# Norm scale and shift, and the MLP's 96x96 weight, computed by GpSimd instead of VectorE

## The chip, the cores and the metric

The kernel runs on one core of one Trainium2 chip. The metric is the device time of one execution in microseconds (us), lower is better. The chip's engines in the profile are PE (TensorE matmul), PEld (its weight loads), DVE (VectorE), ACT (ScalarE), POOL (GpSimd) and SP (SyncE, which here issues the DMAs). Each engine works through its own instructions in order; semaphores hold an instruction back until what it needs is done.

## The reference

Four residual layers on an image batch x of 8 x 48 x 48 x 96, all in float32. Ahead of each stands a group norm with 32 groups of 3 channels:

```python
def _gn(v, G=32, eps=1e-5):
    B_, H_, W_, C_ = v.shape
    g = v.reshape(B_, H_, W_, G, C_ // G)
    m = jnp.mean(g, axis=(1, 2, 4), keepdims=True)
    s = jnp.var(g, axis=(1, 2, 4), keepdims=True)
    return ((g - m) / jnp.sqrt(s + eps)).reshape(v.shape)

x = x + L0(_gn(x))   # selective scan in four directions over the image
x = x + L1(_gn(x))   # upsample, MLP 96 -> 384 -> 96 with a quadratic, low-pass, downsample
x = x + L2(_gn(x))   # four selective scans, each along single rows or columns
x = x + L3(_gn(x))   # as L0, with other weights
return x
```

A selective scan keeps 16 states for each of 192 channels, h = exp(dt A) h + dt u B, and its output is the sum over the states of h C. It is most of the work: 4 directions x 192 channels x 16 states x 2304 positions for each image in each of three layers.

## The kernel before, in words

The batch's images go one after another through three stages that run on the whole core: `ss2d` for layer 0 ("l0", to about 5.9 ms), `lines` for layer 2 (to about 11.9 ms) and `ss2d` for layer 3 ("l3"). Layer 1, the MLP, has no stage of its own. It is a guest (class `Guest`): a generator of small steps that is given a turn in each slot of the scans of l0 and lines, when it has a free PSUM bank.

A stage is driven by `scans`. For each image and each of four directions it goes through five blocks of 480 or 384 positions. A block has four turns of two slots; a turn makes three scans of two units each. The order of the instructions is written out by hand. In a turn t the emission is:

- `scan(t, 0)` on VectorE (L331), the recurrence in place in the tile dbu, with the decays ps_da in PSUM;
- on GpSimd the second product h times C of the turn before (`make_hc`, L337);
- products dt u B for the next turn (`make_dbu`, L299), on VectorE with a copy of B in PSUM (ps_b, copied by ScalarE in L280), and for certain slots a share of them on GpSimd with B in SBUF (bc);
- `scan(t, 1)`, more of the same, then `aside(at)`, which runs the slot's side work;
- `make_hc(t, 0)` on GpSimd, `make_da` (ScalarE's exponentials, L323, into two ps_da buffers), `scan(t, 2)`, and `aside(at + 1)`.

TensorE sums h C over the states (`reduce`, L357 and L359). Side work is what `aside` takes from the generators: the next image's norm and convolution, the finish of the image before, the first projections of later blocks, and the guest's turn.

The norm of an image is `norm_scale` (called by `group_norm` in l0 and l3, whose ScalarE application is L177, and by `front` in lines, application L809). It has six `bn_stats` (L191), one `bn_aggr` (L195), a matmul with gmat that takes the mean over the three channels of a group (L186), a copy of that mean out of PSUM to gm (L200), then dev = (mean - gm)^2 + variance (L202 to L204), seven slots later the same matmul on dev, ScalarE's square root to rs (L210), the reciprocal (L212), and shift = -gm rs (L214). All of dev, gm, rs and shift are 96 partitions by one column. It runs once for each image and stage, 24 times; the first of each stage runs before the stage's scans begin. The guest has its own norm for each of 8 images: gm copied by ScalarE (L1125), `deviate` (L1113 to L1115), the root (L1130), and `invert` (L1118 reciprocal, L1119 shift, L1120 the 96x96 matrix wl = wlin rs + I, which is used some 700 us later and more). A guest's step that is a "psum" item puts a matmul and the reader of its result; "do" runs a step, "wait" skips slots.

Tiles whose names begin with ps lie in PSUM; the others named here lie in SBUF.

Of the kernel before, what the change touches and what calls it, by code (L numbers as in the profile page):

```python
# [11 lines left out]
ALU = mybir.AluOpType  # L12
# [3 lines left out]
H, W, C = 48, 48, 96  # L16
# [85 lines left out]
def vss_stack_kernel(ctx: ExitStack, tc: tile.TileContext, i: dict, out: bass.AP):  # L102
    nc = tc.nc
# [11 lines left out]
    def weights(pool, names):  # L115
        w = {}
        for name in names:
            shape = list(i[name].shape)
            w[name] = pool.tile(shape, F32, tag=f"w_{name}", name=f"w_{name}")
            nc.sync.dma_start(w[name], i[name])  # L120
        return w

    wc = weights(const, ("gmat", "red"))
# [44 lines left out]
        return t  # L168


    def group_norm(x, into, psum, behind=lambda step: step()):


        got = {}
        yield from norm_scale(x, got, psum, behind)
        for r0, nr in BLKS:
            nc.scalar.activation(into(r0, nr), x[:, r0:r0 + nr, :], AF.Identity, bias=got["shift"], scale=got["rs"])  # L177
            yield True

    def norm_scale(x, got, psum, behind=lambda step: step()):  # L180


        def mean_of(v):
            def run():
                got["p"] = psum()
                nc.tensor.matmul(got["p"][:C, :1], lhsT=wc["gmat"], rhs=v, start=True, stop=True)  # L186
            behind(run)

        st = small.tile([C, 6, nc.vector.BN_STATS_DIM], F32, tag="st", name="st")
        for n in range(6):  # L190
            nc.vector.bn_stats(st[:, n, :], x[:, 8 * n:8 * n + 8, :])  # L191
            if n % 2:
                yield True
        mv = small.tile([C, 2], F32, tag="mv", name="mv")
        nc.vector.bn_aggr(mv, st)  # L195
        yield True
        mean_of(mv[:, 0:1])
        yield
        gm = small.tile([C, 1], F32, tag="gm", name="gm")
        nc.vector.tensor_copy(gm, got["p"][:C, :1])  # L200
        dev = small.tile([C, 1], F32, tag="dev", name="dev")
        nc.vector.tensor_sub(dev, mv[:, 0:1], gm)  # L202
        nc.vector.tensor_mul(dev, dev, dev)
        nc.vector.tensor_add(dev, dev, mv[:, 1:2])  # L204
        for _ in range(7):
            yield True
        mean_of(dev)
        yield
        rs = small.tile([C, 1], F32, tag="rs", name="rs", bufs=2)
        nc.scalar.activation(rs, got["p"][:C, :1], AF.Sqrt, bias=eps5[:C])  # L210
        yield True
        nc.vector.reciprocal(rs, rs)  # L212
        shift = small.tile([C, 1], F32, tag="shift", name="shift", bufs=2)
        nc.vector.scalar_tensor_tensor(shift, gm, -1.0, rs, ALU.mult, ALU.mult)  # L214
        got["rs"], got["shift"] = rs, shift
        yield True

# [292 lines left out]
    def ss2d(l, xin, xout, guest=None):  # L510
# [46 lines left out]
        def front(b):  # L557
            x = xpad[:C, 1:1 + H, 1:1 + W]
            yield from group_norm(x, lambda r0, nr: xpad[:C, 1 + r0:1 + r0 + nr, 1:1 + W], side_psum)
# [213 lines left out]
    def lines(xin, xout, guest):  # L773
# [29 lines left out]
        def front(b, behind=lambda step: step(), wait=()):  # L803
            got = {}
            x = seq(xs[b], False)
            yield from norm_scale(x, got, lambda: ps("sb", 1), behind)
            yield from wait
            for r0, nr in BLKS:
                nc.scalar.activation(shift(rowwise, 0, 0)[:C, r0:r0 + nr, :], x[:, r0:r0 + nr, :], AF.Identity,  # L809
                                     bias=got["shift"], scale=got["rs"])  # L810
                yield True
# [175 lines left out]
    class Guest:  # L987
# [54 lines left out]
        def items(self):  # L1042
# [5 lines left out]
            wlin, wl, bl = self.tile([C, C], "wlin"), self.tile([C, C], "wl"), self.tile([C, 1], "bl")  # L1048
            st, mv = self.tile([C, 6, nc.vector.BN_STATS_DIM], "st"), self.tile([C, 2], "mv")
            gm, dev, rs, shift = (self.tile([C, 1], n) for n in ("gm", "dev", "rs", "shift"))  # L1050
# [46 lines left out]
            for b in range(nb):  # L1097
# [11 lines left out]
                def mean_of(v):  # L1109
                    return lambda p: nc.tensor.matmul(p[:C, :1], lhsT=wc["gmat"], rhs=v, start=True, stop=True)  # L1110

                def deviate():
                    nc.vector.tensor_sub(dev, mv[:, 0:1], gm)  # L1113
                    nc.vector.tensor_mul(dev, dev, dev)
                    nc.vector.tensor_add(dev, dev, mv[:, 1:2])  # L1115

                def invert():
                    nc.vector.reciprocal(rs, rs)  # L1118
                    nc.vector.scalar_tensor_tensor(shift, gm, -1.0, rs, ALU.mult, ALU.mult)  # L1119
                    nc.vector.scalar_tensor_tensor(wl, wlin, rs, wc["ident"], ALU.mult, ALU.add)  # L1120

                def load_xt(c0):
                    nc.sync.dma_start(xt, self.xin[b].rearrange("c (h w) -> h c w", w=W)[:, c0:c0 + HC, :])

                yield "psum", mean_of(mv[:, 0:1]), lambda p: nc.scalar.copy(gm, p[:C, :1])  # L1125
                yield "do", lambda: load_xt(0)
                yield "wait", 1
                yield "do", deviate
# [221 lines left out]
```

## Time and profile before

| what | value |
|---|---|
| median of 3 runs | 17480.02 us (17457.32 to 17484.61) |
| the profiled execution | 17467.17 us |
| its span | 17465.4 us |
| mean granted TensorE clock | 0.839 |
| matmuls / instructions | 53740 / 168933 |
| VectorE instructions | 9976 |
| GpSimd instructions | 8015 |

The page of the profile gives for each engine the busy time, its share of the span and the number of instructions. A group line gives the source line, the engine, the operation, the tiles written and read, the shape, a count, then busy us and mean ns of one, and after the bar the idle us of the engine just ahead of these instructions with what ended that idle time. A table of stretches gives start and end, the length, and the busy us and instructions of PE, PEld, DVE, ACT and POOL, then the granted clock, the DMA engines' busy share and GB/s. A timeline line gives start us, length in us, engine, line, operation, tiles, shape and how many instructions are merged in it.

The page's waits show where each engine is held: ScalarE's L323 has 2436.5 us of idle time ahead of it, 2202.9 of it ended by VectorE's scans.

### The profile page before, as it was taken

What the parts mean: (1) busy time and instruction counts of PE and PEld (TensorE: products, weight loads), DVE (VectorE), ACT (ScalarE), POOL (GpSimd) and SP (SyncE); (2) the same over time, 40 slices, a digit from 0 to 9 for tenths busy, and PEclk for the clock granted to TensorE, in tenths of its full rate; (3) what the DMA queues carried; (4) which work ended last, traced back from release to release, by engine and by line L of the source; (5) the groups of instructions that cost most, each with busy time, mean ns of one, the idle gap of its engine ahead of it and who ended that gap; (6) DMA issues with size and microseconds to landing.
All of it is one profiled execution on the core that took longest, in us unless ns stands there. A gap on an engine that the chain in (4) does not pass through costs nothing.

```text
span 17465.4 us, 168933 instructions
## 1 busy us (share of the span) xinstructions
PE 13240.6 (76%) x53740; PEld 4749.1 (27%) x53740; DVE 15969.0 (91%) x9976; ACT 13903.6 (80%) x20972; POOL 15179.8 (87%) x8015
## 2 busy tenths in 40 slices
PE   6778787878787677777777777776777777777776
PEld 1223232333232333233233322222222222222221
DVE  7999999999999799899889999996999999999998
ACT  6878878878787688888788888886878878878776
POOL 7988888988888788888788888886999999999998
PEclk7878888888897888899889888887878878878877
DMA  4554555454555444444444444443555555455454
GB/s 139 179 169 167 174 166 175 169 177 168 165 176 172 135 147 162 147 158 156 153 154 155 153 155 156 153 157 125 173 174 171 176 168 178 171 170 177 169 177 145
DMA packets 887918, 2843.65 MB, mean 163 GB/s; under 512 B 353468, under 2 KB 421788, under 8 KB 760206
## 3 DMA queue, kind: packets, MB, share of 16 engines
q1 hardware_dynamic: 887022, 2832.85, 47.7%
q8 instruction: 422, 6.91, 0.2%
q14 instruction: 474, 3.88, 0.1%
HBM read 2384.40 MB, written 448.17 MB: 162 GB/s over the span
## 4 chain that ended last, share of the span: by engine, by line
DVE 22%; ACT 21%; POOL 19%; issue 14%; PE 13%; DMA 10%; SPq 1%; POOLq 0%; DVEq 0%; ACTq 0%
DVE dbu L331 14%; POOL dbu L337 12%; ACT ps_da L323 7%; DVE dbu L299 6%; POOL dbu L299 5%; DMA dd<-dds 4%; DMA dd<-dd 3%; ACT L323 3%; PE ps_y L357 2%; POOL dds L499 2%; ACT ps_b L280 1%; PE ps_sa L940 1%; PE ps_sa L885 1%; DMA bc<-bcd 1%; ACT L903 1%
## 5 line engine op out<-in xcount | busy, mean ns | idle before, releaser
L331 DVE TENSOR_TENSOR_SCAN dbu<-ps_da,dbu 128x968 f32<-128x968 f32 (+3 forms) x5760 | 11825.2, 2075 | 770.4 <-ACT ps_da L323 610.2
L337 POOL TENSOR_TENSOR dbu<-dbu,bc 128x1440 f32<-128x1440 f32 (+1 forms) x3840 | 10064.7, 2633 | 1941.7 <-DVE dbu L331 1860.2
L323 ACT ACTIVATE ps_da<-dd,w_l_a 128x484 f32<-128x484 f32 (+3 forms) x11520 | 7426.2, 649 | 2436.5 <-DVE dbu L331 2202.9
L357 PE MATMUL ps_y<-dbu,w_red 128*32 128x480 f32 (+1 forms) x23040 | 4253.3, 658 | 1600.6 <-POOL dbu L337 1572.4
L359 PE MATMUL ps_y<-dbu,w_red 128*32 128x480 f32 (+1 forms) x7680 | 4215.2, 657 | 0.0
L299 DVE TENSOR_TENSOR dbu<-dd,ps_b 128x962 f32<-128x962 f32 (+5 forms) x2880 | 3831.5, 1330 | 265.6 <-ACT ps_b L280 156.1
L299 POOL TENSOR_TENSOR dbu<-dd,bc 128x481 f32<-128x481 f32 (+5 forms) x2240 | 3911.2, 1761 | 23.6 <-DMA dd<-dd 19.0
L357 PEld LDWEIGHTS ps_y<-dbu,w_red 128*32 128x32 f32 x23040 | 729.0, 118 | 5033.5 <-POOL dbu L337 3369.4
L280 ACT COPY ps_b<-bc 128x482 f32<-128x482 f32 (+3 forms) x2720 | 1449.2, 533 | 214.7 <-DVE dbu L299 167.3
L574 PE MATMUL ps_side<-xpad,w_l_cw 128*128 128x480 f32 (+1 forms) x2880 | 1342.0, 604 | 48.4 <-ACT g_room L1176 16.9
L323 ACT ACT_TABLE_LOAD x993 | 1274.0, 1283 | 17.8
L703 PE MATMUL ps_s<-bcl,square 128*128 128x480 f32 (+1 forms) x1280 | 888.0, 785 | 323.2 <-ACT dds L707 163.8
L353 PE MATMUL ps_y<-big,eye 128*128 128x480 f32 (+1 forms) x960 | 748.3, 868 | 231.8 <-ACT big L754 227.4
L713 PE MATMUL ps_s<-big,square 128*128 128x480 f32 (+1 forms) x1280 | 849.4, 794 | 65.4 <-ACT g_room L1176 18.5
L499 POOL TENSOR_TENSOR dds<-dds,big 96x960 f32<-96x960 f32 (+1 forms) x320 | 705.9, 2206 | 166.6 <-ACT dds L731 166.2
L574 PEld LDWEIGHTS ps_side<-xpad,w_l_cw 128*128 128x128 f32 x2880 | 570.4, 209 | 804.9 <-issue 696.6
L885 PE MATMUL ps_sa<-ub,square 128*128 128x480 f32 (+1 forms) x640 | 405.0, 770 | 382.9 <-ACT ub L875 382.9
L359 PEld LDWEIGHTS ps_y<-dbu,w_red 128*32 128x32 f32 x7680 | 666.7, 118 | 0.0
L866 PE MATMUL ps_sb<-xpad,square 128*128 128x480 f32 (+1 forms) x1280 | 600.5, 615 | 85.0 <-ACT g_room L1176 31.3
L866 PE MATMUL ps_sa<-xpad,square 128*128 128x480 f32 (+1 forms) x1280 | 538.0, 561 | 0.0
L707 ACT ACTIVATE dds<-ps_s,w_l_dtb 96x480 f32<-96x480 f32 (+1 forms) x640 | 405.1, 633 | 123.4 <-DMA dd<-dds 71.0
L754 ACT COPY big<-ps_y 96x480 f32<-96x480 f32 (+1 forms) x640 | 471.0, 736 | 34.7 <-PE ps_y L359 33.3
(243 smaller groups left out, 12648.2 us busy)
## 6 DMA issues: line engine op xcount, KB each, us to landing
dd<-dd SPq DMA_DIRECT2D x512, 1452.0 KB
bc<-bcd SPq DMA_DIRECT2D x1536, 480.0 KB
dd<-dd SPq DMA_DIRECT2D x256, 1440.0 KB
dd<-dds SPq DMA_DIRECT2D x512, 363.0 KB
dd<-dd SPq DMA_DIRECT2D x128, 1164.0 KB
bc<-bcd SPq DMA_DIRECT2D x384, 384.0 KB
dd<-dds SPq DMA_DIRECT2D x256, 360.0 KB
dd<-dd SPq DMA_DIRECT2D x64, 1152.0 KB
```

The costliest lines, as they stand in the source:

```text
L280: nc.scalar.copy(bps[t][:, :bcs[t][0].shape[1]], bcs[t][0])
L299: engine.tensor_mul(o, du, by.unsqueeze(1).to_broadcast([P, hi - lo, by.shape[1]]))
L323: nc.scalar.activation(da[:, at:at + b.m], b.got[half][:, u % 3, 0, :], AF.Exp, scale=a[:, b.k, ci:ci + 1])
L331: nc.vector.tensor_tensor_scan(db, da, db, 0.0, ALU.mult, ALU.add)
L337: nc.gpsimd.tensor_mul(h, h, bcs.pop(2 * t + sub)[1].unsqueeze(1).to_broadcast([P, 3, n]))
L357: nc.tensor.matmul(y[32 * g:32 * g + 32, :n], lhsT=wc["red"][:, :32], rhs=hc[:, g, b.at], start=False, stop=(slot == 3))
L359: nc.tensor.matmul(y[DH:, :n], lhsT=wc["red"][:, 32:], rhs=hc[:, 2, b.at], start=False, stop=(slot == 3))
L499: nc.gpsimd.tensor_mul(du, dt, u)
L574: nc.tensor.matmul(pu[:, :n], lhsT=flat[:, at:at + P], rhs=xpad[:, r0 + dy:r0 + dy + nr, dx:dx + W], start=(tap == 0), stop=(tap == 8))
L703: nc.tensor.matmul(got["p"][:, :n], lhsT=wide("dtw", (2 * b.k + half) * DH), rhs=b.bcl[:, :n], start=True, stop=True)
L713: nc.tensor.matmul(got["p"][:, :n], lhsT=wide("xp", (2 * b.k + half) * NBC), rhs=uall[:, half], start=(half == 0), stop=(half == 1))
L866: nc.tensor.matmul(got["u", half][:, :n], lhsT=wide("cw", at), rhs=shifted(off), start=(tap == 0), stop=(tap == 3))
```

## The change

Nine operations of VectorE for the norms are issued on GpSimd. A new helper holds three of them. gm holds the negative mean (the copy becomes a multiplication by -1, on VectorE in the norms and on ScalarE in the guest), so that the difference becomes a sum and the shift a plain product. wl, one instruction on VectorE before, is two on GpSimd: a product with rs broadcast along the row, and the sum with the identity. The reciprocals stay on VectorE.

```diff
+    def spread(dev, mv, gm):
+
+        nc.gpsimd.tensor_add(dev, mv[:, 0:1], gm)
+        nc.gpsimd.tensor_mul(dev, dev, dev)
+        nc.gpsimd.tensor_add(dev, dev, mv[:, 1:2])
+
     def group_norm(x, into, psum, behind=lambda step: step()):
...
         gm = small.tile([C, 1], F32, tag="gm", name="gm")
-        nc.vector.tensor_copy(gm, got["p"][:C, :1])
+        nc.vector.tensor_scalar(gm, got["p"][:C, :1], -1.0, None, ALU.mult)
         dev = small.tile([C, 1], F32, tag="dev", name="dev")
-        nc.vector.tensor_sub(dev, mv[:, 0:1], gm)
-        nc.vector.tensor_mul(dev, dev, dev)
-        nc.vector.tensor_add(dev, dev, mv[:, 1:2])
+        spread(dev, mv, gm)
...
         nc.vector.reciprocal(rs, rs)
         shift = small.tile([C, 1], F32, tag="shift", name="shift", bufs=2)
-        nc.vector.scalar_tensor_tensor(shift, gm, -1.0, rs, ALU.mult, ALU.mult)
+        nc.gpsimd.tensor_mul(shift, gm, rs)
...
                 def deviate():
-                    nc.vector.tensor_sub(dev, mv[:, 0:1], gm)
-                    nc.vector.tensor_mul(dev, dev, dev)
-                    nc.vector.tensor_add(dev, dev, mv[:, 1:2])
+                    spread(dev, mv, gm)
 
                 def invert():
                     nc.vector.reciprocal(rs, rs)
-                    nc.vector.scalar_tensor_tensor(shift, gm, -1.0, rs, ALU.mult, ALU.mult)
-                    nc.vector.scalar_tensor_tensor(wl, wlin, rs, wc["ident"], ALU.mult, ALU.add)
+                    nc.gpsimd.tensor_mul(shift, gm, rs)
+                    nc.gpsimd.tensor_mul(wl, wlin, rs.to_broadcast([C, C]))
+                    nc.gpsimd.tensor_add(wl, wl, wc["ident"])
...
-                yield "psum", mean_of(mv[:, 0:1]), lambda p: nc.scalar.copy(gm, p[:C, :1])
+                yield "psum", mean_of(mv[:, 0:1]), lambda p: nc.scalar.mul(gm, p[:C, :1], -1.0)
```

## The prediction

> **What bounds the kernel now.** I read the page first: the busy shares and the two costliest groups.
>
> ```profile
> span 17465.4 us, 168933 instructions
> PE 13240.6 (76%) x53740; PEld 4749.1 (27%) x53740; DVE 15969.0 (91%) x9976; ACT 13903.6 (80%) x20972; POOL 15179.8 (87%) x8015
> L331 DVE TENSOR_TENSOR_SCAN dbu<-ps_da,dbu 128x968 f32<-128x968 f32 (+3 forms) x5760 | 11825.2, 2075 | 770.4 <-ACT ps_da L323 610.2
> L337 POOL TENSOR_TENSOR dbu<-dbu,bc 128x1440 f32<-128x1440 f32 (+1 forms) x3840 | 10064.7, 2633 | 1941.7 <-DVE dbu L331 1860.2
> ```
>
> VectorE is the busiest, and GpSimd's idle time is nearly all waiting for VectorE's scans. An average over three stages hides much, so next I asked for busy time by stage (l0, lines, l3):
>
> ```profile
> 100.00:5850.00 5750.00, 4527.64 (x19671) 1734.13 (x19673) 5275.76 (x3248) 4618.15 (x7190) 5069.37 (x2843) 0.84 0.52 170
> 5950.00:11900.00 5950.00, 4519.45 (x18248) 1719.53 (x18246) 5425.97 (x3475) 4898.87 (x7147) 4910.64 (x2237) 0.88 0.43 154
> 12000.00:17400.00 5400.00, 3974.01 (x15134) 1195.20 (x15134) 5183.81 (x3154) 4279.99 (x6468) 5047.09 (x2836) 0.80 0.50 172
> ```
>
> The third busy column is VectorE: 92%, 91% and 96%. The fifth is GpSimd: 88%, 83% and 93%. Then the groups of VectorE, for the lines that the change takes away:
>
> ```profile
> L203 DVE TENSOR_TENSOR dev<-dev 96x1 f32<-96x1 f32 x24 | 38.8, 1616 | 0.8
> L202 DVE TENSOR_TENSOR dev<-mv,gm 96x1 f32<-96x1 f32 x24 | 29.6, 1235 | 0.8
> L214 DVE SCALAR_TENSOR_TENSOR shift<-gm,rs 96x1 f32<-96x1 f32 x24 | 27.4, 1141 | 0.8
> L204 DVE TENSOR_TENSOR dev<-dev,mv 96x1 f32<-96x1 f32 x24 | 21.3, 886 | 0.8
> L1113 DVE TENSOR_TENSOR g_dev<-g_mv,g_gm 96x1 f32<-96x1 f32 x8 | 12.3, 1537 | 2.9 <-ACT g_gm L1125 2.9
> L1119 DVE SCALAR_TENSOR_TENSOR g_shift<-g_gm,g_rs 96x1 f32<-96x1 f32 x8 | 10.9, 1367 | 0.3
> L1120 DVE SCALAR_TENSOR_TENSOR g_wl<-g_wlin,g_rs,eye 96x96 f32<-96x96 f32 x8 | 9.6, 1201 | 0.0
> L1115 DVE TENSOR_TENSOR g_dev<-g_dev,g_mv 96x1 f32<-96x1 f32 x8 | 9.6, 1196 | 0.3
> L1114 DVE TENSOR_TENSOR g_dev<-g_dev 96x1 f32<-96x1 f32 x8 | 8.6, 1080 | 0.3
> ```
>
> One column costs 1.1 to 1.6 us on average, while the reciprocal L212 of the same size takes 0.135 us. The mean hides two kinds: the shortest of L202, L203 and L204 take 154 ns, the longest 2.66 us. The timeline of VectorE, then GpSimd, at one norm shows why:
>
> ```profile
> 16342.81 1.31 DVE L202 TENSOR_TENSOR dev<-mv,gm 96x1 f32<-96x1 f32 x1
> 16344.16 2.66 DVE L203 TENSOR_TENSOR dev<-dev 96x1 f32<-96x1 f32 x1
> 16346.85 0.15 DVE L204 TENSOR_TENSOR dev<-dev,mv 96x1 f32<-96x1 f32 x1
> 16346.93 4.24 DVE L331 TENSOR_TENSOR_SCAN dbu<-ps_da,dbu 128x968 f32<-128x968 f32 x2
> 16340.37 3.74 POOL L299 TENSOR_TENSOR dbu<-dd,bc 128x481 f32<-128x481 f32 x2
> 16344.07 2.73 POOL L337 TENSOR_TENSOR dbu<-dbu,bc 128x1440 f32<-128x1440 f32 x1
> 16349.18 2.73 POOL L337 TENSOR_TENSOR dbu<-dbu,bc 128x1440 f32<-128x1440 f32 x1 [2.38 <-DVE dbu L331]
> ```
>
> L202 ends at 16344.12, as L299 ends (16344.11); L203 ends at 16346.82, as L337 ends (16346.80); L204 falls where GpSimd is idle and takes 0.15 us. Over the trace, 81 of the 136 moved instructions last over 350 ns; most of the stalled ones end 10 to 20 ns after a GpSimd instruction does, the 96-column L1120 some 110 ns after.
>
> **What the Trainium skill says.** "SBUF — State Buffer", section "Who interferes with whom": a VectorE instruction with two SBUF inputs contends with a GpSimd instruction that reads SBUF, the later one waits for the whole of the other, and one with a single SBUF input doesn't contend. The trace agrees: the ends above coincide, while the scans and L299 on VectorE, whose other operand is in PSUM, run beside GpSimd at steady durations. "GPSIMD Engine Reference", section "3.1 Elementwise — side-by-side cycle accounting": about 156 ns dispatch for an instruction, 2.6 cycles an element for two inputs. The trace gives L299 on GpSimd 1035 ns at 481 columns and 2737 ns at 1440, so 1.77 ns an element and 0.18 us fixed; I use these. "Perfetto Trace Analysis", section "Optimizing Scalar/DVE Operations", warns that moving work between these two engines might not help, as they share a read port; that is a rival below.
>
> **The change part by part.** *VectorE loses* 4 instructions in each of 24 norms (L202, L203, L204, L214) and 5 in each of 8 images of the guest (L1113 to L1115, L1119, L1120): 136 instructions. The sum of the nine rows is 38.8+29.6+27.4+21.3+12.3+10.9+9.6+9.6+8.6 = 168.1 us. Gaps add nothing: durations overlap the next start slightly (from L202's start to the scan's is 4.12 us, the sum of the three durations). By stage, adding the same rows within each, 77.3 us lie in l0, 58.2 in lines, 32.6 in l3; 0.6 of each belongs to the stage's first norm, where nothing runs beside it.
>
> *How much of that is on the path.* I compare blocks (12 scans each, first scan to first scan). In l3 the block with L202 to L204 lasts 39.0 us in six images and 32.7 in the last, which has no norm to do: 6.3 us more, for 4.1 us of moved and 2.6 us of other norm work, 94%. In l0 the same pair (the sixth image against the last) is 39.8 against 32.9, 6.9 for 6.7, all of it, but with the guest's work mixed in; I take 90%. In lines it is 39.4 against 36.5, 2.9 for 4.5, 65%. Lines has a cleaner pair: at 7751 us L214 stalls for 2.74 us, at 9259 us it takes 0.15. From the reciprocal's start to L931's is 12.67 us in one and 11.45 in the other: a stall of 2.59 us cost 1.22, 47%, because ACT's table loads held the next scans anyway and caught up. I take 60% for lines. So 76.7 x 0.90 + 57.6 x 0.60 + 32.0 x 0.94 = 69 + 35 + 30 = 134 us.
>
> *GpSimd gains* 128 operations of one column at about 0.19 us (0.18 fixed; its five-column copy L311 takes 0.192) and 16 of 96x96 at 0.18 + 96 x 0.00177 = 0.35: 24 + 6 = 30 us. No such operation on GpSimd is in the trace; bounds are 0.11 us (its memset L308) and 0.5 us (fixed part, dispatch and a dependent start each time), 16 to 75 us. There is no gain to be had from an added operation itself, so the low end isn't below nothing. GpSimd idles 2286 us, so this hides in its waits for scans; if that cover were gone it would cost the 30.
>
> *New waits on GpSimd.* dev now waits in its queue for gm, shift for the reciprocal; behind them stand the products L337, for which TensorE's L357 waits, and later its share of L299. I laid the changed order over the old times. In l3 GpSimd comes to its place 1.33 us after gm is ready and 3.0 after the reciprocal: no wait. In lines it comes about 0.35 early. Counting only what lies beyond the time at which GpSimd would have gone on, the waits sum to 13 us, the longest 1.6. As VectorE comes earlier these shrink, and GpSimd's idle of 2.4 us behind that norm takes them; I charge half, 6. The readers: TensorE's second mean comes 26.7 us after dev in l3; ACT's L177 comes 5.2 us after shift there, and GpSimd is 3.0 + 0.2 late, so 2 us remain. The guest's second mean comes 0.1 to 18 us after; there GpSimd is up to 2.6 us late but the old chain, stalled up to 5.7 us, wasn't earlier.
>
> *Small rest.* gm's copy becomes a multiply from PSUM, one input, 0.13 us as before (bounds -0.05 to +0.05 on 24, 1 us). The three bare norms cost about 0.5 more each for hops between engines, 1.5 us. No DMA is added or moved.
>
> **Sum.** 134 - 6 - 1.5 = 126 us. The profiled execution took 17467.2 (span 17465.4 and 1.8 around it), which gives 17341; the median shown is 12.9 above it, so 17480 - 126 = 17354. Once VectorE is relieved, ACT's ps_da (610 us of waits) is late next, as before.
>
> **The rivals.**
> - *Absorbed* (0.17): l0 behaves like lines, since the guest loads ACT and TensorE there too: 60% in l0, 30% in lines, 94% in l3 is 46 + 17 + 30, less 8: 85, so 17395. For it: ACT is the releaser of most scan waits. Against: idle time of VectorE in the 10 us after a stall is mostly nothing in l0.
> - *All of it* (0.08): every stall is on the path and waits vanish: 17480 - 168 = 17312. Against: the pair in lines.
> - *Given back* (0.05): the shared port makes GpSimd or another stall equal; no VectorE operation left with two SBUF inputs is in the loop, which speaks against it. 17480.
> - *Slower* (0.03): GpSimd's queue in front of L337 becomes the bound. With 13 us of waits and all of GpSimd's added time on the path, it decides from (126 + 6 - 13)/144 = 0.83 us for an added operation; at 1.2 us, 17480 + 54 = 17534. Against: its smallest take 0.1 to 0.2 us.
>
> **How the numbers follow.** The forecast, gain 95 to 165, has 0.67. The range 17300 to 17420 (gain 180 to 60) holds it, the full gain and about half of what is absorbed. The bound of telling from no change is 0.2%, 35 us: faster 0.92, same 0.05, slower 0.03.
>
> **What would show it.** Right: VectorE's busy time down by about 165 us, no such rows there, the new rows on GpSimd near 0.2 and 0.35 us, its idle before L337 down by over 100 us, l3's norm block near 35 us, lines' near 37. Wrong: GpSimd rows near 1 us, scans waiting for GpSimd's dbu, or ACT's wait ahead of L177 or for ps_da growing by tens of us.

## The result, and the profile after

The changed kernel took 17374.7 us (median of 6 runs, 17368.3 to 17385.5) against 17462.2 for the kernel before beside it: a ratio of 0.9947, 95% interval 0.9936 to 0.9957. Timed a second time, with other kernels on another occasion, it took 17370.8 against 17472.4, 0.9942 (0.9930 to 0.9955). So it gains 88 to 102 us, where 126 were forecast. The profiled execution took 17373.8 us.

The page of the changed kernel, for the lines that answer to those shown before:

```profile
span 17371.9 us, 169003 instructions
PE 13193.7 (76%) x53740; PEld 4744.7 (27%) x53740; DVE 15807.2 (91%) x9840; ACT 13897.8 (80%) x20972; POOL 15212.7 (88%) x8159
L335 DVE TENSOR_TENSOR_SCAN dbu<-ps_da,dbu 128x968 f32<-128x968 f32 (+3 forms) x5760 | 11823.5, 2075 | 814.5 <-ACT ps_da L327 653.1
L341 POOL TENSOR_TENSOR dbu<-dbu,bc 128x1440 f32<-128x1440 f32 (+1 forms) x3840 | 10069.9, 2635 | 1775.7 <-DVE dbu L335 1715.3
```

VectorE has 136 instructions fewer and 162 us less busy time. The span fell by 93.5 us only, and the scans' wait for ScalarE's ps_da grew from 610 to 653 us. GpSimd's idle time ahead of the products fell by 166 us. (Lines of the changed kernel are 4 to 6 further down: the scan is L335, the products L341 and L303, dt u L503.)

The stages, from the first scan of one to the first scan of the next (l0 from the start of the span). Columns as before: start and end, length, then busy time of PE, PEld, VectorE, ACT and GpSimd. The kernel before:

```profile
0.00:5970.00 5970.00, 4651.83 (x20058) 1794.03 (x20058) 5317.14 (x3303) 4686.12 (x7300) 5150.83 (x2904) 0.84 0.51 167
5970.00:12022.70 6052.70, 4588.37 (x18412) 1749.58 (x18412) 5433.94 (x3493) 4923.93 (x7184) 4948.04 (x2266) 0.87 0.43 152
12022.70:17465.40 5442.70, 4000.37 (x15270) 1205.46 (x15270) 5217.90 (x3181) 4293.58 (x6490) 5080.90 (x2845) 0.80 0.50 170
```

and the kernel after:

```profile
0.00:5906.20 5906.20, 4636.13 (x20058) 1794.05 (x20058) 5241.12 (x3238) 4683.92 (x7300) 5167.61 (x2976) 0.85 0.52 169
5906.20:11948.30 6042.10, 4592.42 (x18412) 1755.95 (x18412) 5379.80 (x3451) 4922.62 (x7184) 4957.42 (x2310) 0.87 0.43 152
11948.30:17371.90 5423.60, 3965.13 (x15270) 1194.68 (x15270) 5186.28 (x3153) 4291.30 (x6490) 5087.62 (x2873) 0.81 0.50 171
```

In l0 VectorE lost 76 us and the stage 64. In lines VectorE lost 54 us and the stage 10.6. In l3 it lost 32 and the stage 19. In this pair of profiles the missing part of the gain is mostly in lines. The timeline of VectorE and then of GpSimd at the norm in l3 that was shown before is now:

```profile
16247.46 2.16 DVE L335 TENSOR_TENSOR_SCAN dbu<-ps_da,dbu 128x968 f32<-128x968 f32 x1
16249.54 0.13 DVE L206 TENSOR_SCALAR gm<-ps_side 96x1 f32<-96x1 f32 x1
16249.59 4.22 DVE L335 TENSOR_TENSOR_SCAN dbu<-ps_da,dbu 128x968 f32<-128x968 f32 x2
```

```profile
16248.25 2.74 POOL L303 TENSOR_TENSOR dbu<-dd,bc 128x1443 f32<-128x1443 f32 x1
16250.95 0.19 POOL L173 TENSOR_TENSOR dev<-mv,gm 96x1 f32<-96x1 f32 x1
16251.22 0.19 POOL L174 TENSOR_TENSOR dev<-dev 96x1 f32<-96x1 f32 x1
16251.49 0.19 POOL L175 TENSOR_TENSOR dev<-dev,mv 96x1 f32<-96x1 f32 x1
16251.63 5.42 POOL L341 TENSOR_TENSOR dbu<-dbu,bc 128x1440 f32<-128x1440 f32 x2
```

The scans follow gm at once. GpSimd comes to dev 1.3 us after gm is there, as the forecast had it, and the three operations cost it 0.68 us. The blocks of l3 that hold a norm fell from 39.0 to 34.8 us, by 4.2 us, which is all of the stall (4.12 us).

In lines the same place looks different. This is the norm of the fifth image there in the kernel before, VectorE and then dt u on GpSimd:

```profile
9203.25 2.09 DVE L331 TENSOR_TENSOR_SCAN dbu<-ps_da,dbu 128x960 f32<-128x960 f32 x1
...
9212.32 1.51 DVE L202 TENSOR_TENSOR dev<-mv,gm 96x1 f32<-96x1 f32 x1
9213.87 0.15 DVE L203 TENSOR_TENSOR dev<-dev 96x1 f32<-96x1 f32 x1
9214.06 2.66 DVE L204 TENSOR_TENSOR dev<-dev,mv 96x1 f32<-96x1 f32 x1
9216.64 2.14 DVE L331 TENSOR_TENSOR_SCAN dbu<-ps_da,dbu 128x960 f32<-128x960 f32 x1
```

```profile
9211.94 1.88 POOL L499 TENSOR_TENSOR dds<-dds,ub 96x960 f32<-96x960 f32 x1
```

The block begins with the scan at 9203.25. The same point in the kernel after, where the block begins at 9127.06, VectorE first:

```profile
9135.96 0.15 DVE L206 TENSOR_SCALAR gm<-ps_sb 96x1 f32<-96x1 f32 x1
9137.78 2.16 DVE L335 TENSOR_TENSOR_SCAN dbu<-ps_da,dbu 128x960 f32<-128x960 f32 x1 [1.68 <-ACT ps_da L327]
...
9157.86 1.65 DVE L303 TENSOR_TENSOR dbu<-dd,ps_b 128x1440 f32<-128x1440 f32 x1 [1.56 <-DMA dd<-dd]
```

and GpSimd:

```profile
9136.18 0.19 POOL L173 TENSOR_TENSOR dev<-mv,gm 96x1 f32<-96x1 f32 x1 [0.39 <-DVE gm L206]
9136.45 0.19 POOL L174 TENSOR_TENSOR dev<-dev 96x1 f32<-96x1 f32 x1
9136.72 0.19 POOL L175 TENSOR_TENSOR dev<-dev,mv 96x1 f32<-96x1 f32 x1
9136.86 1.88 POOL L503 TENSOR_TENSOR dds<-dds,ub 96x960 f32<-96x960 f32 x1
```

Where 4.3 us of stall stood, 1.68 us of waiting for ps_da remain; 20 us later 1.56 us of waiting for the load of dd are new. What dd holds comes from dds, which L503 (dt u) computes on GpSimd. L503 starts 9.8 us after the block's first scan, 1.1 us later than before (8.7), since dev stands ahead of it. That gave two questions: is the wait of VectorE's two-input operations what was paid for, and what ate the gain in lines, GpSimd's queue or the other engines?

### The profile page after: what moved, and what is told of

Its sections match the earlier page's. It is cut to its first block, busy times and chain, and to the rows that moved or that the text cites. A ratio compares the mean times of both kernels' runs of the same rounds, so it can differ in the third digit from the quotient of the medians.

```text
span 17371.9 us, 169003 instructions
## 1 busy us (share of the span) xinstructions
PE 13193.7 (76%) x53740; PEld 4744.7 (27%) x53740; DVE 15807.2 (91%) x9840; ACT 13897.8 (80%) x20972; POOL 15212.7 (88%) x8159
## 4 chain that ended last, share of the span: by engine, by line
ACT 22%; DVE 21%; POOL 19%; issue 14%; PE 13%; DMA 10%; SPq 1%; POOLq 0%; DVEq 0%; ACTq 0%
DVE dbu L335 14%; POOL dbu L341 12%; ACT ps_da L327 8%; DVE dbu L303 6%; POOL dbu L303 4%; DMA dd<-dds 4%; DMA dd<-dd 3%; ACT L327 3%; PE ps_y L361 2%; POOL dds L503 2%; ACT ps_b L284 1%; PE ps_sa L944 1%; PE ps_sa L889 1%; DMA bc<-bcd 1%; ACT L907 1%
## 5 line engine op out<-in xcount | busy, mean ns | idle before, releaser
L335 DVE TENSOR_TENSOR_SCAN dbu<-ps_da,dbu 128x968 f32<-128x968 f32 (+3 forms) x5760 | 11823.5, 2075 | 814.5 <-ACT ps_da L327 653.1
L341 POOL TENSOR_TENSOR dbu<-dbu,bc 128x1440 f32<-128x1440 f32 (+1 forms) x3840 | 10069.9, 2635 | 1775.7 <-DVE dbu L335 1715.3
L361 PE MATMUL ps_y<-dbu,w_red 128*32 128x480 f32 (+1 forms) x23040 | 4206.5, 651 | 1588.0 <-POOL dbu L341 1554.0
L363 PE MATMUL ps_y<-dbu,w_red 128*32 128x480 f32 (+1 forms) x7680 | 4168.0, 651 | 0.0
L303 DVE TENSOR_TENSOR dbu<-dd,ps_b 128x962 f32<-128x962 f32 (+5 forms) x2880 | 3831.0, 1330 | 286.1 <-ACT ps_b L284 157.3
L303 POOL TENSOR_TENSOR dbu<-dd,bc 128x481 f32<-128x481 f32 (+5 forms) x2240 | 3913.5, 1762 | 22.5 <-DMA dd<-dd 18.2
L503 POOL TENSOR_TENSOR dds<-dds,big 96x960 f32<-96x960 f32 (+1 forms) x320 | 706.7, 2209 | 144.9 <-ACT dds L735 144.6
```

Source lines behind the costliest of these rows:

```text
L303: engine.tensor_mul(o, du, by.unsqueeze(1).to_broadcast([P, hi - lo, by.shape[1]]))
L335: nc.vector.tensor_tensor_scan(db, da, db, 0.0, ALU.mult, ALU.add)
L341: nc.gpsimd.tensor_mul(h, h, bcs.pop(2 * t + sub)[1].unsqueeze(1).to_broadcast([P, 3, n]))
L361: nc.tensor.matmul(y[32 * g:32 * g + 32, :n], lhsT=wc["red"][:, :32], rhs=hc[:, g, b.at], start=False, stop=(slot == 3))
L363: nc.tensor.matmul(y[DH:, :n], lhsT=wc["red"][:, 32:], rhs=hc[:, 2, b.at], start=False, stop=(slot == 3))
L503: nc.gpsimd.tensor_mul(du, dt, u)
```

## The experiments

Theory: VectorE's two-input operations waited for GpSimd's reads; their removal gains in full where VectorE is the bound (l0, l3) and little in lines. Rivals: GpSimd's new waits eat the rest; or the removed instructions themselves were what counted. Stage lengths below are from the first scan of a stage to that of the next, in us, from one profile each; before had 5854, 6053 and 5443 (l0 from its first scan), the change 5791, 6042 and 5424, and in its second profile 5800, 6042 and 5422.

### The kernel before once more

No edit.

> The kernel before, unchanged, profiled a second time, to see how much a block of 12 scans varies from one execution to the next. The theory (a stall of VectorE on GpSimd's reads is what the change removes, and what the blocks without a norm show is jitter) expects a span within 15 us of 17465, blocks of l3 that hold a norm within 0.3 us of the first profile, and blocks at the start and end of l3's images that differ by 1 to 2 us as they do between before and after. The rival (those blocks pay something back for the change) expects them the same in both profiles of before, within 0.3 us.

Measured: one run of 17486.7, at the upper edge of before's 17458 to 17488. Stages 5861, 6063 and 5446: 6.5, 10.6 and 3.4 longer than in the first profile of the same code. The norm blocks of l3 are within 0.3 us; the second block of an image, 34.9 in the first profile in images two to eight, here is 34.9 to 35.8. So whole stages wander by some 10 us, the norm blocks of l3 don't, and the small losses at the start of l3's images are at least in part jitter. It also says that the change in lines, 10.6 us, is of the size of that jitter. Part of what wanders is the stall itself: L214 took 40.7 us in all here and 27.4 in the first profile, with 8 us of the difference in lines.

### VectorE in forms with one tensor input

```diff
-        nc.vector.tensor_sub(dev, mv[:, 0:1], gm)
-        nc.vector.tensor_mul(dev, dev, dev)
-        nc.vector.tensor_add(dev, dev, mv[:, 1:2])
+        nc.vector.tensor_scalar(dev, mv[:, 0:1], gm, None, ALU.subtract)
+        nc.vector.tensor_scalar(dev, dev, dev, mv[:, 1:2], ALU.mult, ALU.add)
...
-        nc.vector.scalar_tensor_tensor(shift, gm, -1.0, rs, ALU.mult, ALU.mult)
+        nc.vector.tensor_scalar(shift, gm, rs, -1.0, ALU.mult, ALU.mult)
```

The guest's dev and shift are changed in the same way. Its wl goes to GpSimd, as in the change.

> The arithmetic of dev and shift stays on VectorE, in forms with one tensor input and one-column operands as per-partition scalars: dev in two instructions, shift in one, 96 instructions in all; wl on GpSimd as in the change. The theory (what was paid for is the wait for GpSimd's reads, not the instruction) expects no instruction of these over 0.25 us, about 14 us of them in all, and a time 75 to 95 us below before, so within 15 us of the change. A rival, that GpSimd's new waits for gm and the reciprocal eat some 40 us of the change's gain, expects it 100 to 140 us below before. A second rival, that one-column scalars are read through the shared port too, expects the stalls to stay and at most 25 us of gain.

Measured: 17369.6 against 17472.7, 0.9942 (0.9930 to 0.9955), a gain of 103 us. VectorE's groups:

```profile
L203 DVE TENSOR_SCALAR dev<-dev,mv 96x1 f32<-96x1 f32 x24 | 6.5, 269 | 0.9
L202 DVE TENSOR_SCALAR dev<-mv,gm 96x1 f32<-96x1 f32 x24 | 5.0, 210 | 0.8
L213 DVE TENSOR_SCALAR shift<-gm,rs 96x1 f32<-96x1 f32 x24 | 5.0, 209 | 0.9
```

The shortest and longest of each differ by at most 3 ns in the norms: none ever waited, though 76 of the 96 (with the guest's) lie wholly inside a GpSimd instruction of over 1 us. Of the moved operations only wl left VectorE here, and the gain is that of the change. So the instructions themselves weren't what counted, and 22 us of them on VectorE cost no more in total than what GpSimd's queue cost. The sum was off in one respect: they took 22 us where 14 were expected, and the longest 0.27 us where 0.25 was the limit.

### GpSimd's side alone

```diff
         nc.vector.tensor_add(dev, dev, mv[:, 1:2])
+        nc.gpsimd.tensor_add(idle, mv[:, 0:1], gm)
+        nc.gpsimd.tensor_mul(idle, idle, idle)
+        nc.gpsimd.tensor_add(idle, idle, mv[:, 1:2])
...
         nc.vector.scalar_tensor_tensor(shift, gm, -1.0, rs, ALU.mult, ALU.mult)
+        nc.gpsimd.tensor_mul(idle, gm, rs)
```

and the same in the guest, with wl.

> VectorE does all that it did before, and GpSimd does the change's operations as well, in the same places, into a column that nobody reads (wl is written again with the same values): what GpSimd's side of the change costs by itself. The theory expects 0 to 15 us above before (30 us of added work on GpSimd, hidden in its waits for the scans). The rival, that GpSimd's waits stand in front of dt u and of the products with C and are what ate a third of the forecast gain, expects 25 to 45 us above before.

Measured: 17398.0 against 17472.7, 0.9958 (0.9946 to 0.9971), 75 us faster than before. Both sides were wrong, in sign. VectorE's old instructions are all there, and this is what they take:

```profile
L203 DVE TENSOR_TENSOR dev<-mv,gm 96x1 f32<-96x1 f32 x24 | 20.3, 848 | 0.8
L218 DVE SCALAR_TENSOR_TENSOR shift<-gm,rs 96x1 f32<-96x1 f32 x24 | 18.1, 756 | 0.8
L205 DVE TENSOR_TENSOR dev<-dev,mv 96x1 f32<-96x1 f32 x24 | 4.1, 171 | 0.8
L204 DVE TENSOR_TENSOR dev<-dev 96x1 f32<-96x1 f32 x24 | 3.7, 155 | 0.8
```

The square (here L204) took 1616 ns before and takes 155. GpSimd now has its three small operations to do before its next 2.7 us product, and VectorE's second and third instruction run beside those. In l0 and l3 the first still meets a long instruction that was running; in lines, where GpSimd waits in its queue for gm, the first has no wait either (1.2 us for all eight norms, 10.5 before). The nine groups add up to 60 us instead of 168. So this didn't measure GpSimd's cost; it showed the stall a second time, from the other side.

### The norms alone, the guest alone

The change with the guest's edits taken back, and the change with only those.

> Only the 24 norms of the three stages are moved to GpSimd; the guest's eight keep VectorE. VectorE loses 117 us of busy time. If the share of the stalls that counts is 83% in l0, 20% in lines and 90% in l3, as the stages' lengths before and after say, the gain is 44 x 0.83 + 39 x 0.2 + 32 x 0.9, less some 10: 60 to 65 us. If all stalls count alike at 87/168, 61 us too; the stages then tell them apart, lines gaining 20 us in that case and under 10 in the first. If the guest brings nearly all, under 30.

> Only the guest's eight norms and wl are moved to GpSimd; the 24 norms of the stages keep VectorE. VectorE loses 51 us, 32 of them in l0. With the norms alone at 50 us of gain and the parts adding up, 37 to 43 us below before, most of it in l0. If the parts overlap (either one lets the other stall longer), 20 to 30.

Measured: norms 17419.3 against 17472.7, 0.9971 (0.9960 to 0.9983); guest 17417.3 against 17472.4, 0.9969 (0.9956 to 0.9981). That is 53 and 55 us, 108 together against the change's 88 to 102, but 117 us of busy time bring 53 and 51 bring 55. The stages: norms alone 5833, 6045 and 5420; guest alone 5819, 6036 and 5446. In l0 the guest's edits gain 36 us for the 32 that they take off VectorE there, the norms' 21 for 45; in lines the norms gain 8 for 39. In l0 two places of the norms differ. The block that holds dev fell from 40.3 to 36.8 us (mean of the second to the seventh image), 3.5 for a stall of 4.0. The next block, where shift stalled for 2.3 us, fell from 38.4 to 38.1 only, and to 36.2 with the guest's edits alone. So l0 absorbs too, at shift.

### VectorE's time put back, in lines and in l0 with l3

```diff
         gm = small.tile([C, 1], F32, tag="gm", name="gm")
         nc.vector.tensor_scalar(gm, got["p"][:C, :1], -1.0, None, ALU.mult)
         dev = small.tile([C, 1], F32, tag="dev", name="dev")
+        for n in range(again):
+            nc.vector.bn_stats(st[:, n % 6, :], x[:, 8 * (n % 6):8 * (n % 6) + 8, :])
         spread(dev, mv, gm)
```

with again = 8, in lines also behind the reciprocal, in each norm that runs beside the scans.

> The change, with work put back on VectorE where the stalls of lines were: in seven norms of lines, 8 more bn_stats (0.54 us each, one SBUF input, results not used) behind gm and 8 more behind the reciprocal, 14 places of 4.3 us, 60.5 us in all. The theory (in lines VectorE's time is mostly not on the path: loads of dd, TensorE and ACT are late there too) expects 10 to 25 us above the change. The forecast's share of 60% expects 36; if VectorE bounds lines as it does l3, 55 to 60.

> The change, with the same 8 bn_stats behind gm in seven norms of l0 and seven of l3, also 14 places of 4.3 us, 60.5 us in all. The theory (there VectorE is the bound) expects 50 to 62 us above the change, and the blocks of l3 that hold a norm 4.2 us longer each. If the third of the gain that is missing is lost everywhere alike, 30 to 40.

Measured: in lines 17385.9 against 17475.5, 0.9949 (0.9937 to 0.9962); in l0 and l3 17424.9 against 17475.5, 0.9970 (0.9958 to 0.9981). The groups added, first in lines (two places), then in l0 and l3:

```profile
L209 DVE BATCH_NORM_STATS2 st<-x 96x6 f32<-96x384 f32 x56 | 26.3, 540 | 0.0
L221 DVE BATCH_NORM_STATS2 st<-x 96x6 f32<-96x384 f32 x56 | 26.3, 539 | 0.0
```

```profile
L209 DVE BATCH_NORM_STATS2 st<-xpad 96x6 f32<-96x384 f32 x112 | 52.8, 541 | 0.0
```

Neighbours overlap, so both doses are 53 us and not 60.5. In l0 and l3 they cost 50 to 54 us over the change by the medians (40 to 49 by the ratios), and 3.6 us in each norm block of l3. In lines they cost 11 to 15 us by the medians, 3 to 12 by the ratios, and the stage is 6043 long, 1.3 more than the change's. So in l0 and l3 VectorE is the bound at the places behind gm, and in lines it mostly isn't at either place.

### Lines without the change, and with it in another way

Three kernels that differ from the change in the norms of lines only. In the first these keep VectorE's two-input form; in the second they have the one-input forms; in the third dev stays on GpSimd but is issued a slot later:

```diff
+        if later:
+            yield True
         spread(dev, mv, gm)
-        for _ in range(7):
+        for _ in range(6 if later else 7):
             yield True
```

> The change, with dev and shift of the eight norms of lines left on VectorE in the two-input form, with their stalls (about 39 us before); l0, l3 and the guest on GpSimd. The theory (removing stalls in lines gains little) expects 0 to 12 us above the change. The forecast's 60% expects 23. If GpSimd's 1.1 us ahead of dt u in lines costs more than the stalls do, it comes out below the change by 5 to 15.

> The change, with the norms of lines in one-input forms on VectorE (two instructions for dev, one for shift, about 0.69 us a norm together): no stall and nothing ahead of GpSimd's dt u in lines. If GpSimd's place in the queue costs something in lines, 5 to 12 us below the change; if not, within 5 us of it. Against the kernel with all norms in one-input forms it should be 5 to 10 below, since l0 and l3 keep VectorE free of these 10 us.

> The kernel with one-input forms in lines and GpSimd elsewhere, beside the change this time. If GpSimd's work ahead of dt u in lines costs something, 8 to 20 us below the change, all of it in lines; if the difference seen so far was only between chips or runs, within 5 us.

> The change, with the three operations of dev in the norms of lines issued one slot later, so that they stand behind dt u (L503) of the next block in GpSimd's queue and not ahead of it. If the 1.1 us by which dt u was late is what lines lost, it comes out 8 to 15 us below the change, like the kernel with one-input forms in lines. If lines is simply not bound by VectorE or GpSimd there, within 5 us of the change.

> The change itself, timed again beside the next three on the same chip. Expected at 0.9945 to 0.9950 of before, and in its profile the three stages within 12 us of the first profile's 5791, 6042 and 5424.

| kernel | time | ratio | 95% | length of lines |
|---|---|---|---|---|
| lines keeps the old form | 17376.1 | 0.9943 | 0.9929 to 0.9957 | 6044.6 |
| one-input forms in lines | 17359.3 | 0.9934 | 0.9922 to 0.9947 | 6029.0 |
| the same again | 17360.2 | 0.9934 | 0.9922 to 0.9947 | 6029.3 |
| dev a slot later | 17356.4 | 0.9938 | 0.9925 to 0.9952 | 6024.7 |
| the change again | 17370.8 | 0.9942 | 0.9930 to 0.9955 | 6042.1 |

By the time and by the stage, moving the norms of lines to GpSimd is worth nothing against keeping their stalls, 39 us of them. Its two relatives, without stalls and without dev ahead of dt u, are 10.6 and 14.5 us below it on the same chip. Those differences lie within the intervals of the whole, so I read the stage: 6042.1 twice, 6029.0, 6029.3 and 6024.7, 13 to 17 us. Two kernels shown earlier share the code of lines: the one with time put back in l0 and l3 has the change's and took 6037.9, the one-input kernel took 6032.1, and that makes it 6 to 17. Nearly the same code in lines (old norms, guest moved) gave 6044.6 and 6035.8, so 9 us are jitter, and the stage alone doesn't decide. GpSimd's order in the third kernel is as meant, dev behind dt u and the next product:

```profile
9131.00 1.88 POOL L505 TENSOR_TENSOR dds<-dds,ub 96x960 f32<-96x960 f32 x1
...
9135.73 2.73 POOL L305 TENSOR_TENSOR dbu<-dd,bc 128x1440 f32<-128x1440 f32 x1
9138.42 0.18 POOL L173 TENSOR_TENSOR dev<-mv,gm 96x1 f32<-96x1 f32 x1
```

VectorE's waits for loads of dd within lines (total us, times, longest), in the kernel before:

```profile
DVE dbu L299 <- DMA dd<-dd: 46.8, 43, 3.5
```

in the change, together with its wait for ScalarE:

```profile
DVE dbu L335 <- ACT ps_da L327: 266.4, 246, 2.9
DVE dbu L303 <- DMA dd<-dd: 58.9, 46, 3.8
```

with dev a slot later, and then with one-input forms:

```profile
DVE dbu L305 <- DMA dd<-dd: 51.2, 52, 5.5
```

```profile
DVE dbu L310 <- DMA dd<-dd: 47.7, 48, 3.5
```

That is 12 us more of waiting for dd in the change (9.5 in its second profile) and 1 to 4 in the others. These totals wander too: the kernel before has 49.6 in its second profile, and the kernel with the norms alone moved, dev ahead of dt u, has 50.2.

The blocks of lines that hold a norm decide it more sharply. There are seven, each followed by the block in which shift is computed. Added up over the seven images:

| norms of lines | profiles | wait for dd in the norm's block | that block and the next |
|---|---|---|---|
| stalls kept, guest moved | 2 | 0 | 551 to 554 |
| the change | 3 | 11.8 to 12.8 | 548 to 549 |
| no stall, no dev ahead of dt u | 4 | 3.1 to 5.6 | 540 to 543 |

The table is in us. Its second row holds the two profiles of the change and the kernel with time put back in l0 and l3; its last row holds the one-input kernel, the two profiles with one-input forms in lines and dev a slot later. Dt u mostly starts 8.5 us after the block's first scan in the first and the last row, and 9.6 or later in every image of the change. So dev ahead of dt u costs 5 to 9 us in these blocks. Without it the removal gains 8 to 14 us, and with it 2 to 6, for stalls of 32 to 39 us. The next block alone is half a microsecond longer in the last two rows than in the first: there the gain is given back.

## Why the prediction was right or wrong

The direction and the mechanism were right and the time lay in the range. The gain was a fifth to a third smaller than forecast: 126 forecast, 88 and 102 measured. The first of these is as near to the rival "absorbed" (85) as can be told, so the range held for both and the time alone doesn't speak for the forecast; the stages do, in part.

- *The stall.* Right. VectorE's busy time fell by 162 us (165 forecast). The Trainium skill's "SBUF — State Buffer", section "Who interferes with whom", held in both experiments: the one-input forms never waited, and every two-input instruction that was held up ended just behind a GpSimd instruction (in the kernel before, 78 on one column 9 to 48 ns behind, the four on 96 columns 112 to 117). The page excepts from its rule for one input the modes in which a VectorE instruction uses two ports; nothing of that kind showed here. The warning of the Trainium skill's "Perfetto Trace Analysis", section "Optimizing Scalar/DVE Operations", that moving work between these two engines might not help, didn't come true: on GpSimd the one-column operations took 181 to 208 ns each, so none was held up.
- *GpSimd's operations.* Right. 0.19 us for a column as forecast, 0.35 and 0.385 for 96x96. Busy time rose by 33 us (30).
- *The share in l0, 90%, 69 us.* The two profiles have 64 and 55, five others with the same l0 46 to 61: too high by a fifth on average. What the sum missed is at least shift, whose stalls in l0, 14 us, hardly counted. The rival's 60%, 46 us, is the lower end of these.
- *The share in l3, 94%, 30 us.* The blocks with a norm gave all of it, 4.2 us each in six images and 4.4 in the first, 29.6 in all. The stage fell by 19 and 20.5, in other kernels with the same l3 by 23 to 27. The rest of l3, 5162.5 and 5165.8 us in the two profiles of before, was 5165 to 5173 in the others. What gave back up to 11 us there stays open; jitter is part of it.
- *The share in lines, 60%, 35 us.* This is the step that failed: it gave 10.6 in the first pair of profiles, and 11 to 25 over all profiles of the two codes. The forecast had two pairs, a stall of L214 that cost 47% and a block that seemed to show 65%. It took the higher end, though in the block pair VectorE's other waits differed too, and it didn't look at the block behind, which gives some of it back. In fact lines has several things late at once: behind the removed stall the scan waits 1.68 us for ps_da, and 53 us of VectorE's time put back at 14 places cost 3 to 15 us. The rival "absorbed" had 30% for lines, which is nearer.
- *The new waits on GpSimd, 6 us.* Incompletely named. The text listed the products L337 and L299 as what stands behind dev. In lines it is dt u, L499, whose result goes through two DMAs before VectorE needs it. By the norm's blocks this costs 5 to 9 us, by the stage 6 to 17. That the charge of 6 is near this is luck, since it was worked out for other waits. The rest of what is missing in lines is absorption, which the time put back there shows, with jitter of some 10 us.
- *What would be late next.* Named rightly, ps_da; the sum has no term for it other than the shares below 100%. Its waits grew by 43 us, and the text had listed growth by tens of us as a sign of being wrong.

The lowest times are those of the change with either of the two edits in lines, 17356 to 17360 us, ratio 0.9934 to 0.9938. Their intervals overlap with the change's; that they are faster rests on the blocks of lines.

## What to carry to other kernels

A VectorE instruction on one column that takes microseconds may be held up by GpSimd's reads, as 78 were here; compare its end with GpSimd's ends before thinking of its work. The cheapest cure may be another form on the same engine, with the second operand as a per-partition scalar, rather than another engine and its queue. When moving something into a queue, list what stands behind it by the instruction order at that very place in each stage, and price a stage's gain by what VectorE waits for right behind the removed stall and in the block after it, not by the engine's busy share.

## What the runs showed of the hardware

- A one-column tensor_scalar with one per-partition scalar from SBUF took 209 ns, with two 269 ns, and 76 of 96 lay wholly inside a GpSimd instruction of over 1 us. A tensor_tensor on the same columns took 155 ns undisturbed and up to 2660 ns disturbed. Scalars read that way did not contend.
- Three operations of 0.19 us each on GpSimd, ahead of its next 2.7 us product, freed VectorE's second and third instruction beside them: their mean fell from 1616 and 886 ns to 155 and 171, with more work on GpSimd and 75 us less time.
